# Attention over a 64x64 image on one core: the fifth load of k behind the first energies, the reciprocals' DMA one step later, the sum's halves earlier

## The chip, the cores and the metric

The kernel runs on one core of a Trainium2 chip. The metric is the device time of one execution in microseconds; the kernel before takes 2503.32 us, the median of three runs between 2499.98 and 2505.54. Profiles and traces each show one execution. Engines are named as in the profile: PE is TensorE (its weight loads are PEld), DVE is VectorE, ACT is ScalarE, POOL is GpSimd, SP is SyncE. POOL and SP issue the DMAs; each works through its own instructions in order, as the other engines do.

## The reference

There are 4 images of 64x64 pixels with 256 channels, all float32. The reference computes, for each image, self-attention over N = 4096 positions and adds the input:

```python
q = jnp.einsum('bwhc,cd->bwhd', x, Wq) + bq      # C2 = 128 channels
k = jnp.einsum('bwhc,cd->bwhd', x, Wk) + bk
v = jnp.einsum('bwhc,cd->bwhd', x, Wv) + bv      # C = 256 channels
pq = q.reshape(B, -1, N)                         # the layout is reinterpreted:
pk = k.reshape(B, -1, N)                         # 128 (256 for v) rows of 4096
pv = v.reshape(B, -1, N)
energy = jnp.einsum('bcn,bcm->bnm', pq, pk)
attention = jax.nn.softmax(energy, axis=-1)
out = jnp.einsum('bcm,bnm->bcn', pv, attention)
return gamma * out.reshape(B, W, H, C) + x
```

## The kernel before

**Precision.** Matmuls run on a reduced float32 format (F32R). To keep the precision, each operand of the large matmuls is split in forms: a rounded-down high part h and two remainders l and d, made from the float32 value by one ACT operation and two DVE operations. Each product is then three matmuls. The forms of q and k are written together in a tile f (lines 257 to 263), those of v in vh, vl, vd, those of the exponentials in h and ld.

**Projection.** The work on an image b begins with 16 steps i. A step loads x(i) (L82, on SP, three buffers), transposes it on PE (L123), copies it out of PSUM on ACT (L129), multiplies by Wq and Wk (L136) and Wv (L157), adds the bias of q and k on DVE (L145), makes f by one ACT operation (L259) and two DVE operations (L261), and makes v and its forms (L166, L279 on ACT, L283 on DVE). f has two buffers. POOL stores f to DRAM in three DMAs: kf (L264) and two of qd (L266). From step 3 on, the PSUM tiles of a step (transposes, q and k, v) go round four banks a0, a1, b0, b1.

**The overlap of projection and attention.** The function begin (line 472) puts the first loads and energies of the attention into the later steps of the projection: k_0 to k_4 are loaded back from DRAM by load_k (L296, on POOL, four buffers) at i = 4 to 8, q_0 by load_q (L290) at i = 6, the first energies are at i = 10 to 14. energy(b, 0) at i = 11 is the last reader of k_0, whose buffer k_4 takes.

**Attention.** There are 8 groups g of 512 queries (NG), and for each 16 units t of 256 keys (NU); u = 16 g + t is the unit's number in the image. In its pass of the loop at line 509, unit u issues for other units ahead: cross (one part of the energies, L308, with ACT's L309) of unit u + 3, energy (the rest, L323, and the exponentials L326) and upper (h, L332) of u + 2, load_k of u + 5, halves (DVE: the running sum L341, then L346 and L348 for ld) of u + 1. For itself it issues attend in two halves j of the channels (L365), which add into the four PSUM banks a0, b0, a1, b1: one a and one b for each half.

**The end of a group.** When t = 15, emptied (line 374) copies the four banks to the tile o (L379). sum_forms (line 383) splits the running sum s, which L352 has folded in the unit before, into two forms zf: L388 on ACT, L390 on DVE. finish (line 393) adds them up over the partitions by two matmuls z into bank b0 (L400), copies one row out (L401), and goes on in pieces: each call of proceed() runs every active finish up to its next yield. There is one such call at the end of each unit, and one in each step of the projection. So the finish of an image's last group runs through the next image's projection. Its pieces are: the row to DRAM (L403), back in another shape (L405), the reciprocal and its DMA to DRAM (L407, L408) with the sum of o's two parts (L409), the reciprocals spread to all partitions (L412), a piece with nothing, the multiplication of o (L415), the accumulating load that adds the input (L419, on POOL), a piece with nothing, and the store of the result (L422). L403, L405, L408, L412 and L422 are on SP, as are the loads of x.

The order on each engine is that of the code (manual_schedule); the tiles' dependences set the waits.

Of the kernel before, what the change touches and what calls it, by code (L numbers as in the profile page):

```python
# [13 lines left out]
ALU = mybir.AluOpType  # L14
# [6 lines left out]
def kernel(  # L21
# [36 lines left out]
    nc = tc.nc  # L58
# [118 lines left out]
    NU = NM // 2  # L177
    STEPS = NG * NU
    LOOK = 2
# [19 lines left out]
    with ExitStack() as fast:  # L199
# [26 lines left out]
        def start(pieces):  # L226
            active.append(pieces)
            next(pieces)

        def proceed():  # L230
            for pieces in list(active):
                if next(pieces, StopIteration) is StopIteration:
                    active.remove(pieces)
# [34 lines left out]
        def project_v(b, i):  # L268
            images[b].v(i)
            units[b, "v4", i] = now["v4"]  # L270
            if i < NI - 2:
                for _ in halve_v(b, i):
                    pass
# [14 lines left out]
        def load_q(b, g):  # L288
            t = work.tile([P, NJ, 3, P], F32R, tag="q", name=f"q_{b}_{g}")
            nc.gpsimd.dma_start(t, qd[b, g])  # L290
            loads[b, "q", g] = t

        def load_k(b, u):
            if u < STEPS:
                t = kpool.tile([P, 2, 3, P], F32R, tag="k", name=f"k_{b}_{u}")
                nc.gpsimd.dma_start(t, kf[b, u % NU])  # L296
                loads[b, "k", u] = t

        def forms(b, u, i, f):
            return loads[b, "k", u][:, i, f, :], loads[b, "q", u // NU][:, :, f, :]  # L300

        def cross(b, u):

            if u >= STEPS:
                return
            for i in range(2):
                e = units[b, "e", u, i] = ps_e.tile([P, NB], F32, tag="e", name=f"e_{b}_{u}_{i}")
                nc.tensor.matmul(e, *forms(b, u, i, 2), start=True, stop=False, skip_group_check=True)  # L308
                nc.scalar.mul(e, e, -1.0 / (1.0 + E))  # L309

        def energy(b, u):

            if u >= STEPS:
                return
            if u % NU:
                x = ppool.tile([P, 2, NB], F32, tag="x", name=f"x_{b}_{u}", bufs=3)
            else:
                x = ppool.tile([P, 2, NB], F32, tag="s", name=f"s_{b}_{u // NU}")
            units[b, u] = x
            for i in range(2):  # L320
                e = units.pop((b, "e", u, i))
                for f in range(2):
                    nc.tensor.matmul(  # L323
                        e, *forms(b, u, i, f), start=False, stop=(f == 1), skip_group_check=True
                    )
                nc.scalar.activation(x[:, i, :], e, AF.Exp, scale=(1.0 + E) / E)  # L326

        def upper(b, u):
            if u >= STEPS:
                return  # L330
            h = ppool.tile([P, 2, NB], F32R, tag="h", name=f"h_{b}_{u}", bufs=3)
            nc.scalar.activation(h, units[b, u], AF.Identity, scale=UPPER)  # L332
            units[b, u] = units[b, u], h
# [49 lines left out]
        def sum_forms(b, g):  # L383

            s = now["sum"]
            f = work.tile([P, 2, NB], F32R, tag="r", name=f"zf_{b}_{g}", bufs=1)
            h, l = now["z"] = f[:, 0, :], f[:, 1, :]
            nc.scalar.activation(h, s[:, 0, :], AF.Identity, scale=UPPER)  # L388
            yield
            nc.vector.tensor_tensor(l, s[:, 0, :], h.bitcast(F32), ALU.subtract)  # L390
            yield

        def finish(b, g, o, s):
            n = b * NG + g
            r4 = rall[:, n, :]
            row = lambda t: t[n : n + 1, :]
            spread = lambda t: row(t).rearrange("o (p j) -> (o p) j", j=NJ)
            zp = ps_o.tile([P, NB], F32, tag="b0", name=f"z_{b}_{g}")
            for f, x in enumerate(now["z"]):
                nc.tensor.matmul(zp, ones_r, x, start=(f == 0), stop=(f == 1))  # L400
            nc.scalar.copy(s[0:1, 0, :], zp[0:1, :])  # L401
            yield
            nc.sync.dma_start(row(zd), s[0:1, 0, :])  # L403
            yield
            nc.sync.dma_start(r4, spread(zd))  # L405
            yield
            nc.vector.reciprocal(r4, r4)  # L407
            nc.sync.dma_start(spread(rd), r4)  # L408
            nc.vector.tensor_tensor(o[:, 0], o[:, 0], o[:, 1], ALU.add)  # L409
            yield  # L410
            r = work.tile([P, NB], F32, tag="r", name=f"r_{b}_{g}", bufs=1)
            nc.sync.dma_start(r, rd[n, :].partition_broadcast(P))  # L412
            yield
            yield
            nc.vector.tensor_tensor(  # L415
                o[:, 0], o[:, 0], r.unsqueeze(1).to_broadcast([P, 2, NB]), ALU.mult
            )
            yield
            nc.gpsimd.dma_start(o[:, 0], xg[b, g], accum_op=ALU.add)  # L419
            yield  # L420
            yield
            nc.sync.dma_start(og[b, g], o[:, 0])  # L422
# [48 lines left out]

        def begin(b, i):

            if i in (4, 5, 6, 7, 8):
                load_k(b, i - 4)
            if i == 6:
                load_q(b, 0)
            if i in (11, 13):
                energy(b, (i - 11) // 2)
            if i in (10, 11, 13):  # L480
                cross(b, (i - 9) // 2)
            if i in (12, 14):
                upper(b, i // 2 - 6)

        image(0)
        for b in range(B):
            pr = images[b]
            if b == 0:
                now["banks"] = energies
                pr.transposed(0)  # L490

                wp = ps_o.tile([P, P], F32, tag="b1", name="wp1")
                for _ in range(2):
                    nc.tensor.matmul(wp, ones, ones, start=True, stop=True)
                pr.transposed(1)
                project_qk(b, 0)
            for i in range(1, NI):
                if i == 3:
                    now["banks"] = outputs
                if i + 1 < NI:  # L500
                    pr.transposed(i + 1)
                begin(b, i)
                project_qk(b, i)
                if i == NI - 1:
                    halves(b, 0)
                project_v(b, i - 1)
                proceed()
            project_v(b, NI - 1)
            for u in range(STEPS):
                g, t = divmod(u, NU)  # L510
                final = (b, u) == (B - 1, STEPS - 1)
                if t == 6 and g + 1 < NG:
                    load_q(b, g + 1)
                if u == STEPS - NU and b + 1 < B:
                    image(b + 1)
                if u >= STEPS - 3 and b + 1 < B:
                    now["banks"] = energies
                    if u == STEPS - 3:
                        images[b + 1].load(0)
                    elif u == STEPS - 2:  # L520
                        images[b + 1].transposed(0)
                if (b, u) == (B - 1, STEPS - 6):
                    xr = ppool.tile([P, 2, NB], F32, tag="s", name="xr")
                    nc.sync.dma_start(xr, xg[b, g])

                beside = iter(())
                if u in (2, 6):
                    beside = halve_v(b, NI - 2 + u // 4)
                elif t == NU - 1 and not final:
                    beside = sum_forms(b, g)  # L530
                    total = now["sum"]
                cross(b, u + LOOK + 1)
                if not final:
                    attend(b, u, 0)
                    if t == NU - 1:
                        emptied(b, g, 0)
                energy(b, u + LOOK)
                next(beside, None)
                upper(b, u + LOOK)
                load_k(b, u + LOOK + 3)  # L540
                halves(b, u + 1)
                next(beside, None)
                if final:
                    finish_last(b, u, xr)
                    break
                attend(b, u, 1)
                if t == NU - 1:
                    emptied(b, g, 1)
                    start(finish(b, g, now["o"], total))
                else:  # L550
                    proceed()
            if b + 1 < B:
                images[b + 1].transposed(1)
                project_qk(b + 1, 0)
                proceed()
# [134 lines left out]
```

## Time and profile before

| what | value |
|---|---|
| runs shown | 2503.32 us median, 2499.98 to 2505.54 |
| profiled execution | 2508.35 us, span 2506.6 us |
| busy PE, PEld | 2417.9 us (96%), 1980.8 us (79%) |
| busy DVE, ACT, POOL | 2072.6 us (83%), 1854.0 us (74%), 429.2 us (17%) |
| granted TensorE clock, mean | 0.983 |
| DMA, mean over the span | 135 GB/s |

The span in 40 equal slices shows the four images; a digit is the busy share of a slice in tenths:

```profile
PE   8999999999799999999979999999997999999998
PEclk9999999999899999999989999999998999999999
DMA  8444444443754444444385444444438444444443
```

The dips of PE, and the peaks of DMA, are the four projections, at the slices 1, 11, 21 and 31. The rest is the attention, where PE is busy over 90% of the time. Lines of a timeline give the start in us, the duration in us, the engine, the line and operation, and the tile written and read; in brackets stands the idle time of the engine before and what ended it. A line of stretches gives the stretch and its length, the busy time of PE, PEld, DVE, ACT and POOL (with instructions), the granted clock, the busy share of the DMA engines and GB/s. A line of the waits gives the total in us, the number and the longest.

### The profile page before, as it was taken

What the parts mean: (1) busy time and instruction counts of PE and PEld (TensorE: products, weight loads), DVE (VectorE), ACT (ScalarE), POOL (GpSimd) and SP (SyncE); (2) the same over time, 40 slices, a digit from 0 to 9 for tenths busy, and PEclk for the clock granted to TensorE, in tenths of its full rate; (3) what the DMA queues carried; (4) which work ended last, traced back from release to release, by engine and by line L of the source; (5) the groups of instructions that cost most, each with busy time, mean ns of one, the idle gap of its engine ahead of it and who ended that gap; (6) DMA issues with size and microseconds to landing.
All of it is one profiled execution on the core that took longest, in us unless ns stands there. A gap on an engine that the chain in (4) does not pass through costs nothing.

```text
span 2506.6 us, 30467 instructions
## 1 busy us (share of the span) xinstructions
PE 2417.9 (96%) x10588; PEld 1980.8 (79%) x10588; DVE 2072.6 (83%) x2058; ACT 1854.0 (74%) x3071; POOL 429.2 (17%) x781
## 2 busy tenths in 40 slices
PE   8999999999799999999979999999997999999998
PEld 7788888888678888888867888888886888888886
DVE  5888888888588888888858888888885888888887
ACT  4777777777377777777637777777764777777775
POOL 3211111110321111111032111111113211111110
PEclk9999999999899999999989999999998999999999
DMA  8444444443754444444385444444438444444443
GB/s 244 148 119 121 119 125 119 134 128 98 229 155 120 120 126 118 124 129 128 99 237 151 124 119 123 111 130 124 129 105 241 144 128 126 119 122 116 127 124 90
DMA packets 155215, 338.22 MB, mean 135 GB/s; under 512 B 23471, under 2 KB 56751, under 8 KB 155054
## 3 DMA queue, kind: packets, MB, share of 16 engines
q0 software_dynamic: 114656, 293.52, 43.2%
q1 hardware_dynamic: 39854, 42.41, 5.7%
q8 instruction: 87, 1.43, 0.2%
q14 instruction: 74, 0.61, 0.1%
q10 hardware_dynamic: 544, 0.26, 0.0%
HBM read 268.89 MB, written 67.24 MB: 134 GB/s over the span
## 4 chain that ended last, share of the span: by engine, by line
PE 83%; ACT 6%; issue 4%; DMA 4%; DVE 3%; POOL 1%; SPq 0%; DVEq 0%; ACTq 0%; POOLq 0%
PE a L365 36%; PE b L365 18%; PE e L323 17%; PE e L308 9%; DMA qd<-f 2%; ACT o L379 2%; PE qk L136 1%; ACT v L166 1%; DVE zf L390 1%; ACT x L326 1%; PE v L157 1%; DMA x<-in_x_dram 1%; ACT f L259 1%; ACT zf L388 1%; ACT vh L279 1%
## 5 line engine op out<-in xcount | busy, mean ns | idle before, releaser
L326 ACT ACTIVATE x<-e 128x512 f32<-128x512 f32 x960 | 522.3, 597 | 411.1 <-PE e L323 411.1
L341 DVE TENSOR_TENSOR s<-s,x 128x1024 f32<-128x1024 f32 x480 | 587.2, 1223 | 185.3 <-ACT x L326 179.3
L365 PE MATMUL b<-ld,vd 128*128 128x512 f32 x2048 | 635.0, 391 | 2.2 <-DVE ld L348 2.1
L365 PE MATMUL a<-ld,vl 128*128 128x512 f32 x2048 | 631.5, 390 | 5.5 <-DVE ld L346 5.5
L365 PE MATMUL a<-h,vh 128*128 128x512 f32 x2048 | 632.1, 390 | 0.5 <-ACT v L166 0.5
L346 DVE TENSOR_TENSOR ld<-x,h 128x1024 fp32r<-128x1024 f32 x480 | 584.6, 1218 | 3.0 <-DMA qd<-f 3.0
L348 DVE SCALAR_TENSOR_TENSOR ld<-h,x 128x1024 fp32r<-128x1024 f32 x480 | 584.4, 1218 | 0.0
L296 POOL DMA_DIRECT2D k<-kf x512 | 273.7, 535 | 1765.9 <-PE e L323 1584.8
L323 PE MATMUL e<-q,k 128*128 128x512 f32 x2048 | 550.3, 391 | 0.0
L309 ACT ACTIVATE e<-e 128x512 f32<-128x512 f32 x1024 | 544.0, 564 | 0.9 <-PE e L308 0.8
L332 ACT ACTIVATE h<-x 128x1024 fp32r<-128x1024 f32 x480 | 510.0, 1063 | 14.1
L365 PEld LDWEIGHTS b<-ld,vd 128*128 128x128 f32 x2048 | 382.2, 188 | 92.0 <-ACT s L401 9.9
L365 PEld LDWEIGHTS a<-ld,vl 128*128 128x128 f32 x2048 | 384.4, 188 | 87.1 <-DVE ld L346 7.2
L365 PEld LDWEIGHTS a<-h,vh 128*128 128x128 f32 x2048 | 384.7, 188 | 81.4 <-ACT v L166 1.0
L323 PEld LDWEIGHTS e<-q,k 128*128 128x128 f32 x2048 | 384.7, 188 | 80.3
L308 PE MATMUL e<-q,k 128*128 128x512 f32 x1024 | 318.2, 392 | 0.0
L308 PEld LDWEIGHTS e<-q,k 128*128 128x128 f32 x1024 | 192.7, 189 | 38.6
L261 DVE SCALAR_TENSOR_TENSOR f<-f,qks 128x512 fp32r<-128x512 f32 x128 | 82.8, 688 | 95.8 <-ACT f L259 95.8
L259 ACT ACTIVATE f<-qks 128x512 fp32r<-128x512 f32 x64 | 40.4, 632 | 149.0 <-DMA qd<-f 76.6
L136 PE MATMUL qk<-wqk_sb,xts 128*128 128x256 f32 x512 | 138.5, 419 | 0.1
L157 PE MATMUL v<-xts,wv_sb 128*128 128x256 f32 x512 | 121.9, 383 | 0.0
L136 PEld LDWEIGHTS qk<-wqk_sb,xts 128*128 128x128 f32 x512 | 104.9, 213 | 17.6 <-ACT xts L129 2.1
(68 smaller groups left out, 1063.5 us busy)
## 6 DMA issues: line engine op xcount, KB each, us to landing
k<-kf POOLq DMA_DIRECT2D x512, 384.0 KB, 3.4
kf<-f POOLq DMA_DIRECT2D x64, 384.0 KB, 3.2
qd<-f POOLq DMA_DIRECT2D x128, 192.0 KB, 3.7
q<-qd POOLq DMA_DIRECT2D x32, 768.0 KB, 4.9
x<-in_x_dram SPq DMA_DIRECT2D x64, 256.0 KB, 4.7
o<-in_x_dram POOLq DMA_DIRECT2D x31, 512.0 KB, 6.0
out_dram<-o SPq DMA_DIRECT2D x31, 512.0 KB, 3.1
r<-rd SPq DMA_DIRECT2D x31, 256.0 KB, 4.0
```

The lines of the kernel that those rows point to most:

```text
L136: nc.tensor.matmul(qk[:, s, :], self.xt[i][:, k, s, :], wqk_sb[:, k, :], start=(k == 0), stop=(k == KC - 1),)
L157: nc.tensor.matmul(vp[:, eh, :], wv_sb[:, k, eh * P : (eh + 1) * P], self.xt[i][:, k].rearrange("p s a -> p (s a)"), start=(k == 0), stop= ...
L296: nc.gpsimd.dma_start(t, kf[b, u % NU])
L308: nc.tensor.matmul(e, *forms(b, u, i, 2), start=True, stop=False, skip_group_check=True)
L309: nc.scalar.mul(e, e, -1.0 / (1.0 + E))
L323: nc.tensor.matmul(e, *forms(b, u, i, f), start=False, stop=(f == 1), skip_group_check=True)
L326: nc.scalar.activation(x[:, i, :], e, AF.Exp, scale=(1.0 + E) / E)
L332: nc.scalar.activation(h, units[b, u], AF.Identity, scale=UPPER)
L341: nc.vector.tensor_tensor(s, s, x, ALU.add)
L346: nc.vector.tensor_tensor(l, x, h.bitcast(F32), ALU.subtract)
L348: nc.vector.scalar_tensor_tensor(d, h.bitcast(F32), 1.0 + E, x, ALU.mult, ALU.subtract)
L365: nc.tensor.matmul(to, (vh, vl, vd)[f][:, t + NU * i, j * P : (j + 1) * P], units[b, u][f][:, i, :], start=(t == 0 and i == 0 and f != 1), ...
```

## The change

The change has three parts. In finish, the DMA of the reciprocals moves behind a yield of its own, so it is issued one step later, and every later piece too: what follows on SP, DVE and POOL moves by one unit (or by one step of the projection). The sum of o's parts stays where it was. In begin, load_k(b, 4) moves from i = 8 to i = 12. In the loop over units, sum_forms no longer runs beside the unit in two pieces (L388 behind the exponentials, L390 behind halves), but whole, behind cross and ahead of attend.

```diff
@@ finish
             nc.vector.reciprocal(r4, r4)
+            nc.vector.tensor_tensor(o[:, 0], o[:, 0], o[:, 1], ALU.add)
+            yield
             nc.sync.dma_start(spread(rd), r4)
-            nc.vector.tensor_tensor(o[:, 0], o[:, 0], o[:, 1], ALU.add)
             yield
             r = work.tile([P, NB], F32, tag="r", name=f"r_{b}_{g}", bufs=1)
@@ begin
-            if i in (4, 5, 6, 7, 8):
+            if i in (4, 5, 6, 7):
                 load_k(b, i - 4)
             if i == 6:
                 load_q(b, 0)
...
             if i in (10, 11, 13):
                 cross(b, (i - 9) // 2)
+            if i == 12:
+                load_k(b, 4)
             if i in (12, 14):
                 upper(b, i // 2 - 6)
@@ the loop over units
                 beside = iter(())
                 if u in (2, 6):
                     beside = halve_v(b, NI - 2 + u // 4)
-                elif t == NU - 1 and not final:
-                    beside = sum_forms(b, g)
+                cross(b, u + LOOK + 1)
+                if t == NU - 1 and not final:
                     total = now["sum"]
-                cross(b, u + LOOK + 1)
+                    for _ in sum_forms(b, g):
+                        pass
                 if not final:
                     attend(b, u, 0)
```

## The prediction

> **What bounds the kernel now.** I read first the chain of work that ended last, then the waits by engine, the stretches with the granted clock, and last the order of time around the places that the diff touches.
>
> ```profile
> PE 83%; ACT 6%; issue 4%; DMA 4%; DVE 3%; POOL 1%; SPq 0%; DVEq 0%; ACTq 0%; POOLq 0%
> POOL k L296 <- PE e L308: 63.4, 4, 17.6
> ACT f L259 <- DMA qd<-f: 76.6, 15, 12.7
> PE xt L123 <- DMA x<-in_x_dram: 29.3, 7, 6.1
> SPq L408 <- DVE rall L407: 272.2, 31, 11.9
> SPq L422 <- DMA o<-in_x_dram: 526.3, 31, 18.7
> ```
>
> TensorE carries 83% of the chain; the rest lies in a few places. The wait of POOL on L308 comes four times, once per image, up to 17.6 us. SP's waits are long too, but they matter only where something is queued behind them.
>
> ```profile
> 622.00:712.50 90.50, 73.05 (x330) 61.87 (x330) 51.34 (x94) 44.69 (x89) 28.09 (x52) 0.89 0.72 211
> 720.00:780.00 60.00, 59.75 (x264) 49.16 (x263) 54.45 (x50) 46.76 (x78) 8.12 (x16) 1.00 0.38 110
> ```
>
> In the attention loop (second line) TensorE is full at clock 1.00. In the second image's projection (first line) it works 73 of 90.5 us, part of it at a lowered clock, and the DMA engines are busy 0.72 of the time: 65 us of full traffic, a floor for this stretch. So the change is worth what it does to the four projections.
>
> **The fifth load of k.** Call f(i) the DVE pair L261 of step i, x(i) its load, xt(i) its transposes. POOL issues DMAs in order, and k_4 takes the buffer of k_0, which the first energies (begin, i = 11) read last. Before, k_4 stands ahead of kf_8. In image 2:
>
> ```profile
> 683.51 0.53 POOL L296 DMA_DIRECT2D k<-kf  x1 [17.62 <-PE e L308]
> 690.11 0.63 ACT L259 ACTIVATE f<-qks 128x512 fp32r<-128x512 f32 x1 [12.66 <-DMA qd<-f]
> 691.52 1.12 PE L123 MATMUL xt<-ident,x 128*128 128x128 f32 x4 [4.40 <-ACT v L166]
> ```
>
> POOL sits on k_4, kf_8 and kf_9 sit behind it, f(10) waits 12.7 us for f(8)'s buffer, v(9) waits behind f(10) on ACT, and TensorE for v's bank. After the change k_4 is behind qd_11, when the first energies have been run: no wait, and its user, cross(4) in unit 1, is over 10 us away.
>
> Image 1 has nothing else in it, so it gives the price. f(8) ends at 47.14 + 1.29 = 48.43; its DMAs start 0.5 later, take 1.6 to issue and about 4 to land: 54.5. qks(10) is ready at 53.79 + 0.75 = 54.5, so f(10) starts near 55.3 instead of 62.99: 7.7 us earlier. From there TensorE needs, from xt(12) at 54.01, two steps with energies of 5.26 (54.01 to 59.27), two without of 3.89 (17.69 to 21.58 in this image), 3.46 for the last and 1.74 for its v: 23.5, ending at 77.5 where L308 now starts at 84.63. I take **-7.1**.
>
> **The reciprocals' DMA, one step later, in images 2 to 4.** L408 waits on SP for the reciprocal, and x(5) is behind it; L422 waits for the accumulated DMA of L419, and x(11) is behind that:
>
> ```profile
> 636.84 0.33 SPq L408 DMA_DIRECT2D rd<-rall  x1
> 642.00 1.12 PE L123 MATMUL xt<-ident,x 128*128 128x128 f32 x4 [5.92 <-DMA x<-in_x_dram]
> 668.67 0.59 SPq L422 DMA_DIRECT2D out_dram<-o  x1
> 674.77 1.08 PE L123 MATMUL xt<-ident,x 128*128 128x128 f32 x4 [6.12 <-DMA x<-in_x_dram]
> ```
>
> After it the order on SP is x(5), L408, x(6), L412, x(7), ..., x(11), L422, x(12). The blocks are not gone, they stand ahead of x(6), x(7) and x(12). x(6) is issued near 637.3, lands 4.7 later at 642.0; xt(6) would be due one step after xt(5), near 640. The 2 us are hidden: qk(5) ends at 642 + 0.5 + 1.7 = 644.2, and DVE takes it only at 645.9 by its own pace. x(7), behind L412, is the same, just hidden. L415 moves from between f(5) and f(6) to between f(6) and f(7) (1.13 us of DVE either way), L419 from behind qd_6 to behind qd_7, ahead of kf_8.
>
> So the pace of images 2 to 4 is DVE's: f(i) 4.05 us apart when nothing is late (18.86, 22.91, 26.95, 31.00). f(3) to f(15) takes 72.81, 71.80 and 70.94 us before (639.28 to 712.09; 1264.82 to 1336.62; 1887.68 to 1958.62). After:
> - f(3) to f(4): 4.05, with x(5) in time (8.48, 7.97 and 8.59 before).
> - f(4) to f(11): seven steps, 28.35; L415, 1.13; the energies' ACT work ahead of f(11), 0.31 (4.36 against 4.05); and f(8) waiting for f(6), whose stores queue behind q_0's load: 3.45, from image 1 (39.64 to 47.14 less 4.05). Sum 33.2. The traffic gives nearly the same: x 1.8, f 5.5, k 1.6, q 0.8, o 0.5, out 0.5, r 0.3 = 11.0 MB, at 340 GB/s (34 to 47 us, DMA share 1.11) 32.4 us. I take 33.5.
> - f(11) to f(15): as now, 16.95, 17.05, 16.51.
>
> Sums 54.5, 54.6, 54.1: 18.3, 17.2 and 16.8 us less. Off that goes about 1 us because TensorE ends after DVE (as in image 1) and 1 for x(12): L419 issued at f(7)'s stores, near 660, lands 6.8 later, x(12) 5.3 after that, near 672.5, some 2 us after xt(12) is due. I take -16.3, -15.2, -14.8: **-46**. Bounds: -20 each if no wait is left; -8 each if x(12) costs TensorE all that x(11) did (6.1 idle and some 2 of lowered clock).
>
> The clock matters for the short waits that stay. After 4.40 idle it was 0.50 (692 to 697), after 0.99 it stayed 1.00, after 2.64 (to 47.89) it was 0.66 from 48 to 53, a loss of 1.7 us. I put nothing into the sum for two such waits in three images; by the row of 2.64 it would be up to +10, which the range holds. The Trainium skill ("TensorE: Matmul & The Clock Gate", section "Part 1: The HAM clock gate") lets the clock fall after an idle window of about 3.4 us, free-running; by that rule waits of 2 us cost no clock. The row of 2.64 disagrees.
>
> **The sum's halves, made early.** ACT's L388 moves ahead of the L379 pair and the exponentials of a group's last unit, DVE's L390 ahead of L346 and L348.
>
> ```profile
> 222.55 0.49 PE L400 MATMUL z<-zf,ones 128*128 128x512 f32 x1
> 223.28 0.50 PE L400 MATMUL z<-zf,ones 128*128 128x512 f32 x1 [0.23 <-DVE zf L390]
> 224.47 0.56 ACT L401 COPY s<-z 1x512 f32<-1x512 f32 x1
> 225.07 0.30 PEld L365 LDWEIGHTS b<-ld,vd 128*128 128x128 f32 x2 [0.34 <-ACT s L401]
> ```
>
> TensorE loses about 1.1 us here: a group lasts 66.87 (151.85 to 218.80 in the chain), 16 units of 4.08 are 65.3, the two z 0.45. The wait for zf goes. But b0, z's bank, is free only after L401 at 225.03, and ACT runs from 216.57 to 225.97 without a gap, with the same work in either order. TensorE reaches L365 b at 224.08 and waits there 1 us: the stall moves, it doesn't shrink. **0** for 28 boundaries; bounds -31 (1.1 each) and +14 (0.5 each, should the later L348 reach TensorE: it ends near 223.2 instead of 221.1, and b needs it at 225.1). At the three ends of an image with another behind it ACT waits 3.09 us for TensorE before L379, so zf costs it nothing, the two z follow at 620.8 instead of 621.0 and 621.7, and xt(1) starts at 621.3 instead of 622.1: -0.8 each, **-2.4**.
>
> Inside an image L408's DMA keeps its time (SP has nothing else), and L415 and L419 come a unit later; DVE has 0.58 idle in a unit, no k load waits for them that is due within two units: 0.
>
> **Sum:** -7.1 - 46 - 2.4 = -55.5. The profiled execution took 2508.35 (span 2506.6), 5 over the median 2503.3 of the runs; so 2453 for it and **2448** for the median.
>
> **Rivals.**
> 1. The projection runs into its DMAs or keeps its x waits, x(6) or x(12), at full size with the slow clock. For it: the DMA share is 0.98 to 1.09 from 642 to 674. Against it: in image 1 three steps from 22 to 34, at share 1.01, kept 4.05. About -9 for each of three images, -5 for the first: -32, **2471**. The Trainium skill ("DMA: Bandwidth & Descriptors", section "Where 436 GB/s comes from") puts memory's side at some 358 GB/s per core: 11.0 MB would take an estimated 31 us, so by it this rival is no likelier.
> 2. f's buffers keep up everywhere and image ends gain: 20 in three images, 7.7 and 2.4: -70, **2433**.
> 3. Slower: DVE's L390 in front of L346 and L348 holds up unit 16's ld at all 28 boundaries. DVE stands still until ACT has made zf; if ACT took zf only after the exponentials, as now, L348 would end near 225.5, and b would wait 0.4 for it. It decides from 227.2 on, 2.1 us past the point where b needs it, for only then do 28 boundaries eat the 55 and 5 more: **2508**. Against it: L352 ends at 217.7 and ACT has only L309 ahead of L388, so zf is due at 220.3.
> 4. It does nothing, because f(10) waits for something other than the stores behind k_4: 2503. Against it: ACT names the DMA, and image 1 shows it alone.
>
> **Chances.** Forecast 0.52, rival 1 0.26, rival 2 0.17, rival 3 0.03, rival 4 0.02. No change means within 0.2% (5 us), about what a measurement of this kernel can tell. Faster 0.95, same 0.02, slower 0.03. The range 2431 to 2475 reaches to rivals 1 and 2 and the extra clock loss.
>
> **What would show it.** POOL's wait on L308 and ACT's 12 us at L259 gone in all four images; f(3) to f(15) near 54.5; image 1's first L308 of unit 3 at 77 to 78; xt(5) without a wait, xt(12) with about 2 us; at boundaries the waits before L400 gone and L365 b waiting about 1 us for L401. Wrong: a new wait of 5 us or more at xt(6) or xt(12), f(8) or f(9) waiting over 5 us for their DMAs, or a boundary other than 1.6 us over 16 units.

## The result, and the profile after

The changed kernel takes 2466.02 us, the median of four runs between 2465.25 and 2466.45, against 2501.65 for the kernel before in the same comparison: a ratio of 0.9855 with a 95% interval of 0.9838 to 0.9872. That is 36 us less, where 55 had been forecast; 2466 lies inside the range, nearer to the prediction's first rival (2471) than to its forecast (2448). The profiled executions are further apart, 2508.35 and 2466.14 us (spans 2506.6 and 2464.4), since the one of before lies 5 to 7 us above its median; the places below are compared in these two traces, 42.2 us apart.

Three views of the kernel after follow. The first gives the shares of the chain that ended last, by engine; the second some of its waits (total, number, longest); the third the second image's projection as one stretch (PE, PEld, DVE, ACT, POOL busy; clock, DMA share, GB/s).

```profile
PE 80%; ACT 11%; DMA 4%; DVE 2%; issue 1%; POOL 0%; SPq 0%; ACTq 0%; DVEq 0%; POOLq 0%
```

```profile
ACT f L259 <- DMA qd<-f: 36.8, 15, 4.3
PEld b L365 <- ACT s L401: 36.6, 28, 1.3
PE b L365 <- ACT s L401: 24.4, 28, 0.9
PE xt L123 <- DMA x<-in_x_dram: 21.7, 8, 7.2
```

```profile
612.00:691.50 79.50, 69.48 (x330) 59.42 (x329) 51.03 (x94) 45.10 (x89) 28.10 (x52) 0.94 0.80 239
```

POOL's wait on L308 is gone, and ACT's longest wait at L259 has fallen from 12.7 to 4.3 us. The projection lasts 79.5 us instead of 90.5, with the DMA engines busier (0.80). Two lines show what stayed: TensorE now waits 28 times for L401, once at each group end inside an image, and it still waits for x, once for 7.2 us.

The place of that wait in image 2, in the order of time:

```profile
626.99 0.33 SPq L410 DMA_DIRECT2D rd<-rall  x1
631.91 0.63 PE L123 MATMUL xt<-ident,x 128*128 128x128 f32 x4 [1.06 <-DMA x<-in_x_dram]
638.83 0.63 PE L123 MATMUL xt<-ident,x 128*128 128x128 f32 x4 [2.83 <-DMA x<-in_x_dram]
653.34 1.13 POOL L420 DMA_DIRECT2D o<-in_x_dram  x1
659.80 0.59 SPq L423 DMA_DIRECT2D out_dram<-o  x1
666.30 1.09 PE L123 MATMUL xt<-ident,x 128*128 128x128 f32 x4 [5.67 <-DMA x<-in_x_dram]
669.75 2.45 PE L136 MATMUL qk<-wqk_sb,xts 128*128 128x256 f32 x8
677.07 0.54 POOL L296 DMA_DIRECT2D k<-kf  x1
```

xt(5) has no wait any more; xt(6) and xt(7) have short ones. SP stands at the store L423 until the load L420 has landed, x(12) is behind it, and TensorE waits 5.67 us at xt(12). In images 3 and 4 that wait is 7.21 and 3.68 us; for the last of them the view names ACT's L279 in place of x, but it went, too, when the store was moved (below). The multiplication L136 behind it takes 2.45 us, against 1.89 at full clock. k_4 is issued at 677.07 with nothing to wait for.

### The profile page after: what moved, and what is told of

Its sections match the earlier page's. It is cut to its first block, busy times and chain, and to the rows that moved or that the text cites. A ratio compares the mean times of both kernels' runs of the same rounds, so it can differ in the third digit from the quotient of the medians.

```text
span 2464.4 us, 30518 instructions
## 1 busy us (share of the span) xinstructions
PE 2391.0 (97%) x10588; PEld 1973.5 (80%) x10588; DVE 2072.6 (84%) x2058; ACT 1856.3 (75%) x3071; POOL 429.3 (17%) x781
## 4 chain that ended last, share of the span: by engine, by line
PE 80%; ACT 11%; DMA 4%; DVE 2%; issue 1%; POOL 0%; SPq 0%; ACTq 0%; DVEq 0%; POOLq 0%
PE a L365 33%; PE b L365 18%; PE e L323 17%; PE e L308 8%; DMA qd<-f 3%; ACT o L379 3%; ACT h L332 2%; PE qk L136 2%; ACT s L326 1%; ACT x L326 1%; PE v L157 1%; DMA x<-in_x_dram 1%; ACT e L309 1%; ACT v L166 1%; ACT f L259 1%
## 5 line engine op out<-in xcount | busy, mean ns | idle before, releaser
L365 PE MATMUL b<-ld,vd 128*128 128x512 f32 x2048 | 634.6, 391 | 27.1 <-ACT s L401 24.4
L365 PE MATMUL a<-ld,vl 128*128 128x512 f32 x2048 | 631.8, 390 | 3.9 <-DVE ld L346 3.9
L365 PE MATMUL a<-h,vh 128*128 128x512 f32 x2048 | 632.1, 390 | 0.5 <-ACT v L166 0.5
L348 DVE SCALAR_TENSOR_TENSOR ld<-h,x 128x1024 fp32r<-128x1024 f32 x480 | 585.2, 1219 | 0.0
L365 PEld LDWEIGHTS b<-ld,vd 128*128 128x128 f32 x2048 | 381.5, 188 | 119.6 <-ACT s L401 36.6
L365 PEld LDWEIGHTS a<-ld,vl 128*128 128x128 f32 x2048 | 384.4, 188 | 85.6 <-DVE ld L346 5.6
L365 PEld LDWEIGHTS a<-h,vh 128*128 128x128 f32 x2048 | 384.2, 188 | 81.8 <-ACT v L166 1.0
L308 PE MATMUL e<-q,k 128*128 128x512 f32 x1024 | 318.0, 392 | 0.0
L308 PEld LDWEIGHTS e<-q,k 128*128 128x128 f32 x1024 | 192.8, 189 | 40.0
L261 DVE SCALAR_TENSOR_TENSOR f<-f,qks 128x512 fp32r<-128x512 f32 x128 | 82.8, 689 | 60.4 <-ACT f L259 60.4
L136 PE MATMUL qk<-wqk_sb,xts 128*128 128x256 f32 x512 | 127.2, 393 | 0.6 <-ACT xts L129 0.5
L259 ACT ACTIVATE f<-qks 128x512 fp32r<-128x512 f32 x64 | 40.4, 630 | 110.6 <-DVE qks L145 73.8
L157 PEld LDWEIGHTS v<-xts,wv_sb 128*128 128x128 f32 x512 | 98.3, 192 | 15.7 <-PE qk L136 2.0
```

Source lines behind the costliest of these rows:

```text
L136: nc.tensor.matmul(qk[:, s, :], self.xt[i][:, k, s, :], wqk_sb[:, k, :], start=(k == 0), stop=(k == KC - 1),)
L157: nc.tensor.matmul(vp[:, eh, :], wv_sb[:, k, eh * P : (eh + 1) * P], self.xt[i][:, k].rearrange("p s a -> p (s a)"), start=(k == 0), stop= ...
L348: nc.vector.scalar_tensor_tensor(d, h.bitcast(F32), 1.0 + E, x, ALU.mult, ALU.subtract)
L365: nc.tensor.matmul(to, (vh, vl, vd)[f][:, t + NU * i, j * P : (j + 1) * P], units[b, u][f][:, i, :], start=(t == 0 and i == 0 and f != 1), ...
```

## The experiments

f(i) is the DVE pair L261 of step i, as in the prediction. Medians are compared with the kernel before on the same chip, 2504.5 to 2504.7 in the three comparisons. Where a kernel is said to be below the kernel after, it is the difference of the two medians. The kernel after stands in a comparison of its own, in which the kernel before took 2501.65, so such a difference is uncertain by some 3 us.

### The three parts alone

The change has three parts; each was put alone into the kernel before. Only the load:

```diff
-            if i in (4, 5, 6, 7, 8):
+            if i in (4, 5, 6, 7):
                 load_k(b, i - 4)
...
+            if i == 12:
+                load_k(b, 4)
```

> Only the fifth load of k is moved. Theory A (the projections gain from k_4 alone, and x(11) stays blocked behind the store L422): image 1 as with the whole change, its projection 6.9 us shorter and the start of its attention 2.9; in images 2 to 4 x(5) and x(11) still come late, but f(9) to f(10) falls from 18.4, 17.6 and 16.6 us to about 11, so 6 to 8 us each. Sum about -30, median near 2472. Theory B (the yield made the gain of images 2 to 4): only image 1 gains, about -10, median near 2492.

Measured: 2482.83, ratio 0.9907 (0.9889 to 0.9925), -22 us: about midway between the two. The trace sides with A's mechanism: in images 2 to 4 f(3) to f(15) fell by 7.1, 6.0 and 4.3 us, where A had 6 to 8 each and B nothing. f(9) to f(10) fell to 9.7, 9.8 and 9.6 us, further than expected, but f(10) to f(11) grew to 5.3 to 5.4 from 4.4. x(5) and x(11) came as late as before, which TensorE's waits in image 2 show:

```profile
634.66 1.11 PE L123 MATMUL xt<-ident,x 128*128 128x128 f32 x4 [6.33 <-DMA x<-in_x_dram]
667.86 1.09 PE L123 MATMUL xt<-ident,x 128*128 128x128 f32 x4 [7.43 <-DMA x<-in_x_dram]
```

Only the step of the reciprocals' DMA:

```diff
             nc.vector.reciprocal(r4, r4)
-            nc.sync.dma_start(spread(rd), r4)
             nc.vector.tensor_tensor(o[:, 0], o[:, 0], o[:, 1], ALU.add)
             yield
+            nc.sync.dma_start(spread(rd), r4)
+            yield
```

> Only the reciprocals' DMA and what follows it move one step. Theory A: x(5) comes in time, which saves some 3.5 us at f(4) in images 2 to 4, but POOL still stands at k_4, and that wait ends only when the first energies have run behind xt(12), which now waits for x(12) behind the store; what f(4) gains is given back: between -10 and 0, median 2491 to 2502. Theory B: -25, median near 2477.

Measured: 2488.06, ratio 0.9934 (0.9914 to 0.9954), -16.6 us: neither. What f(4) gained (4.4, 3.9 and 4.5 us) was not given back behind k_4: f(9) to f(10) took 15.5, 15.9 and 15.7 us instead of 18.4, 17.6 and 16.6. The two parts add for the most part: in the three images together f(3) to f(15) fell by 17.4 us with the load alone, 17.7 with the step alone and 30.2 with both, 5 less than the sum.

Only the sum's halves:

```diff
-                elif t == NU - 1 and not final:
-                    beside = sum_forms(b, g)
+                cross(b, u + LOOK + 1)
+                if t == NU - 1 and not final:
                     total = now["sum"]
-                cross(b, u + LOOK + 1)
+                    for _ in sum_forms(b, g):
+                        pass
```

> Only the halves of the running sum are made early. Theory A (ACT has no idle time there, the stall of TensorE moves from L400 to L365 b behind L401): at group ends 0.06 to 0.08 us longer each, at the three image ends 0.8 shorter: between -2 and +3 in all, median 2500 to 2505. Theory B (the waits at z were a loss of their own): -1.1 us at 28 boundaries, -31, median near 2471.

Measured: 2503.16, ratio 0.9994 (0.9985 to 1.0004). Theory A: no time of its own. TensorE's waits for zf are gone, and waits of 24.2 us in all at L365 b for L401 stand there instead, as in the kernel after (24.4).

### What holds x(12): the store moved behind the last x

```diff
             nc.gpsimd.dma_start(o[:, 0], xg[b, g], accum_op=ALU.add)
-            yield
-            yield
+            for _ in range(6 if g == NG - 1 else 2):
+                yield
             nc.sync.dma_start(og[b, g], o[:, 0])
```

> The whole change, and in the finish of an image's last group the store of the result is four steps later, behind the last x on SP. Theory A (x(12) was late only because SP stood at the store): TensorE's waits of 5.7, 7.2 and 3.7 us at xt(12) go, and the lowered clock behind them; f(10) to f(11) falls from 11.2, 11.7 and 9.1 to 4.4 to 5: 16 to 19 us less than the whole change, median near 2448. Theory B (the DMA engines are full there, share 1.0, and x(12) or f's buffers would be late anyway): less than 6 us, median above 2460.

Measured: 2450.33, ratio 0.978 (0.9763 to 0.9797), some 16 us below the kernel after. Theory A holds: f(10) to f(11) is 4.36, 4.36 and 4.53 us instead of 11.19, 11.70 and 9.06. In image 2 TensorE goes on without a wait for x(12), and waits 0.33 us for ACT; the store follows later:

```profile
661.17 0.60 PE L123 MATMUL xt<-ident,x 128*128 128x128 f32 x4
662.11 1.22 PE L323 MATMUL e<-q,k 128*128 128x512 f32 x4 [0.33 <-ACT e L309]
662.40 0.67 SPq L423 DMA_DIRECT2D out_dram<-o  x1
```

Whether the other two short waits are worth removing too:

```diff
+            if g == NG - 1:
+                yield
             nc.sync.dma_start(spread(rd), r4)
...
-            yield
-            yield
+            for _ in range(5 if g == NG - 1 else 2):
+                yield
             nc.sync.dma_start(og[b, g], o[:, 0])
```

> The whole change, and in the finish of an image's last group the reciprocals' DMA one step later still and the store behind the last x, so that x(6), x(7) and x(12) are not behind a waiting DMA on SP. Theory A: no wait of TensorE for x above 1 us in images 2 to 4; besides the wait at xt(12) also those at xt(6) (1.1, 0.2, 0.6) and xt(7) (2.8, 1.7, 2.5) go; f(3) to f(15) falls from 61.9, 63.4 and 60.1 us to about 54: 18 to 26 us less than the whole change, median 2440 to 2448. Theory B (the DMA engines' traffic is the bound of steps 4 to 10): f waits for its stores instead, f(3) to f(15) stays above 58: less than 10 us.

Measured: 2455.47, ratio 0.9803 (0.9787 to 0.9819), 10.6 us below the kernel after: just outside theory B's range, far from A's, and not better than moving the store alone (the median is 5 us higher, but the intervals overlap). f(3) to f(15) took 56.8, 56.8 and 57.5 us, between the two theories. TensorE has no waits for x left in the projections, but ACT's waits at L259 for f's buffers are 57.1 us, against 36.8 in the kernel after and 42.3 with the store alone (the first line is the store alone, the second this kernel):

```profile
ACT f L259 <- DMA qd<-f: 42.3, 15, 5.0
```

```profile
ACT f L259 <- DMA qd<-f: 57.1, 19, 4.6
```

So in steps 4 to 10 the next limit, the wait for f's stores, is close behind the x loads. This kernel also differs from the one with the store alone by the input's load, which the extra yield moves from step 7 to step 8. f(10) to f(11) takes 6.55, 6.45 and 7.10 us in it, against 4.36 to 4.53 there: f(11) waits for f(9)'s stores, which now run beside that load. So this run doesn't price the waits at xt(6) and xt(7) by themselves.

### The group end: z and its copy earlier

```diff
-                attend(b, u, 1)
                 if t == NU - 1:
-                    emptied(b, g, 1)
+                    attend(b, u, 1, (0, 1))
                     start(finish(b, g, now["o"], total))
+                    attend(b, u, 1, (2,))
+                    emptied(b, g, 1)
                 else:
+                    attend(b, u, 1)
                     proceed()
```

> The whole change, and in a group's last unit the two matmuls z and the copy L401 stand ahead of the second half's b matmuls and of the second pair of L379, so that ACT reaches L401 some 1.15 us earlier. Theory A (TensorE waits at L365 b for L401 because of what stands ahead of it on ACT): the wait of 0.87 us at 28 boundaries shrinks to 0.3 or less: 15 to 24 us less than the whole change, median 2442 to 2451. Theory B (ACT's sum of work sets the boundary, whatever its order): TensorE then waits as long at another place, within 5 us of the whole change, median 2461 to 2471.

Measured: 2440.42, ratio 0.974 (0.9723 to 0.9756), 26 us below the kernel after: theory A, and a little more than its upper end. L401 now stands ahead of the second pair of L379, and TensorE goes from z to the next unit's b without a wait (ACT, then PE, in the order of time; lines between these are left out):

```profile
215.41 0.56 ACT L401 COPY s<-z 1x512 f32<-1x512 f32 x1
215.88 0.68 ACT L379 ACTIVATE o<-a,gam 128x512 f32<-128x512 f32 x1
```

```profile
213.83 0.62 PE L400 MATMUL z<-zf,ones 128*128 128x512 f32 x2
214.29 0.63 PE L365 MATMUL b<-ld,vd 128*128 128x512 f32 x2
216.14 0.63 PE L365 MATMUL b<-ld,vd 128*128 128x512 f32 x2
216.61 1.09 PE L323 MATMUL e<-q,k 128*128 128x512 f32 x4
```

A group takes 65.96 us (211.66 to 277.62 at L388) against 66.95 after (208.25 to 275.20 at h): 0.99 less, at 28 group ends 28 us, of which the medians show 26.

### Both together

> Both of the two above together. Theory A: they lie in different stretches (group ends; projections), so they add: 33 to 48 us less than the whole change, median 2418 to 2433. Theory B of either: one of them is missing from the sum.

Here the group end's edit stands beside the one that frees x(6), x(7) and x(12). Measured: 2431.63, ratio 0.9708 (0.9693 to 0.9723), 34 us below the kernel after: they add. With the store alone instead:

> The whole change with the store behind the last x and z early. Theory A (projection and group ends are separate): the 16 us of the one and the 25 us of the other add, median 2423 to 2429. Theory B (the start of a projection hangs on the group end before it, so that they share): above 2431.

Measured: 2423.19, ratio 0.9677 (0.9664 to 0.9691), 43 us below the kernel after. Theory A.

### What holds the projection then

Two further kernels took traffic out of the busiest steps, each on top of the one before. First the loads of k, then the input's accumulating load (with it the store of the result goes from step 13 to step 14):

```diff
-            if i in (4, 5, 6, 7):
+            if i in (4, 5):
                 load_k(b, i - 4)
+            if i == 9:
+                load_k(b, 2)
...
-            if i == 12:
-                load_k(b, 4)
+            if i in (12, 13):
+                load_k(b, i - 9)
```

> As the one before, and the loads k_2, k_3 and k_4 stand at steps 9, 12 and 13 instead of 6, 7 and 12, where the DMA engines are less busy. Theory A (after the store is out of the way, steps 5 to 10 are held by the DMA traffic, through f's two buffers): f(5) to f(9) wait less, f(3) to f(15) falls by 1.5 to 3 us in each image, 6 to 12 us in all. Theory B (f waits for the latency of its own three stores, whatever else is on the DMA engines): within 3 us of the one before.

```diff
-            yield
+            for _ in range(6 if g == NG - 1 else 1):
+                yield
             nc.gpsimd.dma_start(o[:, 0], xg[b, g], accum_op=ALU.add)
-            for _ in range(6 if g == NG - 1 else 2):
-                yield
+            yield
+            yield
             nc.sync.dma_start(og[b, g], o[:, 0])
```

> As the one before, and the accumulating load of the input, of the last group of an image, stands five steps later, at step 12 instead of 7, and the store two steps after it. Theory A (traffic): another 1.5 to 3 us in each of images 2 to 4, 4 to 9 us. Theory B: within 3 us.

Measured: 2422.27 (ratio 0.9672, 0.9659 to 0.9685) and 2427.74 (0.9694, 0.9681 to 0.9707). The first is no different, as theory B had it; the second is not faster but 5 us slower in the median, which neither had. The two intervals overlap slightly, but the slowest run of the first (2424.68) is faster than the fastest of the second (2426.93). The traces show that waits moved. Where the input's load left step 7, f(9) to f(10) fell from 6.1, 5.5 and 6.2 us to 4.05 in all three images; where it went, f(14) to f(15) grew from 4.05 to 5.2, 5.3 and 5.9, and TensorE's wait for ld at the start of the attention grew as well. The projections of images 2 to 4 (from the last z to the first L365) became 0.8, 0.4 and 1.6 us shorter, but the attentions became longer, that of image 4 by 3.2 us up to its last z, the other three by 0.8 to 1.4. The page's waits of the first kernel, then of the second:

```profile
ACT f L259 <- DMA qd<-f: 41.6, 16, 3.8
PE a L365 <- DVE ld L346: 6.0, 4, 2.7
```

```profile
ACT f L259 <- DMA qd<-f: 38.9, 14, 3.8
PE a L365 <- DVE ld L346: 9.8, 4, 4.8
```

So f's stores near the moved load were late again: f(15) waits for those of f(13), and ld, which shares its two buffers with f, for those of f(14). Whether the input's load or the result's store delays them, the run doesn't show, since both moved. Whether a third buffer for f would help was not tried. The fastest kernel tried is thus the whole change with the store behind the last x and z early, without these two: 2423 us (2422 with the loads spread, which is not distinguishable).

## Why the prediction was right, and where it was off

**The mechanism was right in the load of k and at the group ends, and right by half in the reciprocals' DMA.** Of the three parts, POOL's block at k_4 was the largest loss (22 us alone), and it is gone in all four images; x(5) is in time; the group ends cost nearly the same. The direction is as forecast, and the median is inside the range. But the range had been drawn to reach the first rival, and what happened at x(12) is what that rival had: the number doesn't confirm the sum. Two of the prediction's own signs failed as well. It named a new wait of 5 us or more at xt(12) as a sign of being wrong, and that wait was 5.7 and 7.2 us in images 2 and 3; and f(3) to f(15) took 61.9, 63.4 and 60.1 us instead of about 54.5.

**The sum was too large.** By the places in the two traces (the first L308 of unit 3, then xt(1) of the next image):

| stretch | forecast | measured |
|---|---|---|
| projection 1 | -7.1 | -6.9 |
| attention 1, with its image's end | -0.8 | -2.9 |
| projections 2, 3, 4 | -16.3, -15.2, -14.8 | -10.9, -10.0, -10.8 |
| attention 2 to 4, with two image ends | -1.6 | -0.7 |
| sum (-55.5 in the prediction's rounding) | -55.8 | -42.2 |

**The step that failed** is the term "1 for x(12)" in the sum of images 2 to 4. f(10) to f(11) took 6.8, 7.3 and 4.7 us more than the 4.36 it takes when nothing is late: some 19 where 3 had been put. Moving the store away gave 16 back, and that kernel, at -54, is where the forecast of -55 had been: its projections 2 to 4 (last z to first L365) are 16.6, 15.8 and 15.9 us shorter than before, where 16.3, 15.2 and 14.8 had been forecast. The agreement is close, but in part luck: f(3) to f(15) fell by 46.1 us in all in that kernel, where the sum had 52.3 before it took off 6 for TensorE's end and x(12). The price was wrong for two reasons, shown here for image 2. The wait of 3.45 for f's buffer had been placed at f(8), but its time was spent sooner: f(5) and f(6) waited for their buffers and came 0.7 and 1.5 us late, f(7), behind xt(7), another 0.9 beside the multiplication of o. So f(4) to f(7) took 16.5 us instead of 13.3, f(7) to f(8) 4.05. The sum from f(4) to f(10), 29.0, was as forecast (28.9), but L420 stands behind f(7)'s stores and left with them, some 3 us later than worked out, and TensorE waited 5.7 us for x(12), not 2. And after that idle time the clock was low, so xt(12), the energies and qk(11) took 5.9 us (666.30 to 672.20), against 4.3 with the store moved away (661.17 to 665.51). The granted clock was 0.57 in the stretch around them:

```profile
664.00:672.00 8.00, 5.70 (x18) 4.84 (x19) 1.19 (x2) 2.76 (x5) 1.58 (x3) 0.57 0.88 276
```

**The rivals.** The first had this, x(12) at its full size with the slow clock, and its 2471 lies nearer than the forecast. Its other half, the DMA traffic, was not what stopped the kernel after, since the store's move alone gave 16 us. The experiments show waits for f's stores as the next limit; how much of them is traffic stays open, since spreading the loads of k gained nothing. The 340 and 358 GB/s that the prediction reckoned with were no upper bound: from 639 to 644 the DMA engines moved 392. The second (no wait left) was ruled out by f's stores: in images 2 to 4 f(3) to f(15) stays at 55.7 to 57.8 us with the store moved and at 56.8 to 57.5 with all of x free, against the 54.5 of the forecast and the 48.6 of twelve steps of 4.05. The third did not happen: at the group ends TensorE's b waits for L401, not for L348. The fourth fell with the trace of the load alone: image 1's f(9) to f(10) went from 11.8 to 5.6 us.

**The group ends** came out as worked out: TensorE's wait is 0.87 us at L365 b instead of about 1.1 around L400, and a group takes 66.95 instead of 66.88 (154.97 to 221.85 at L388). The two ends that the prediction gives for a group are 66.95 apart, not 66.87, which changes nothing in its sum. What the forecast called a fixed sum of ACT's work was a matter of order after all: putting L401 ahead of two copies that are needed later freed bank b0 in time, and saved 0.99 us per group.

**Attention 1** gained 2.1 us more than the image's end. In the kernel before TensorE waited 2.71 us for ld there and then ran at a lower clock (0.66 in the 5 us from 88.6); after, it waits 1.18, and the clock stays 1.00.

## What to carry to other kernels

When an in-order queue blocks on a DMA that must wait, moving that DMA one place chooses which load stands behind it, and the wait can come back there; ask for every later item of the queue what will be late next, with its time counted from the events it really follows, and move the waiting item behind the last load that others need. When a wait moves from one line to another without getting shorter, look at what stands ahead of the releasing instruction on its engine: its order may be the whole cost. Price a wait together with what runs slower after it.

## What the runs showed of the hardware

The clock often fell after short idle times, but the length of the idle time alone didn't decide it. In the kernel after, TensorE idled 2.83 us ahead of xt(7) in image 2 and 2.46 in image 4, and the granted clock was 0.66 and 0.70 in the 5 us that followed; after 1.65 us in image 3 it stayed 1.00. In image 1 of the same kernel it fell to 0.66 (48 to 53) after only 1.90 us. The other way round, with the store alone moved, it stayed 1.00 behind 3.24 us of idle time (image 4, ahead of 1856.75). The clearest pair is in the last kernel, whose input's load is late: ahead of xt(7) TensorE idled 2.85 us in image 2 and 2.84 in image 3, and the clock in the 5 us behind was 0.66 (from 632.5) and 1.00 (from 1234.9). What else decides it, no run here shows. The stretches of the kernel after, image 3 first, then 4, then 2:

```profile
1250.00:1254.00 4.00, 3.83 (x20) 3.38 (x21) 1.32 (x3) 2.05 (x5) 0.17 (x1) 1.00 1.09 336
1866.00:1871.00 5.00, 5.00 (x20) 4.27 (x19) 3.34 (x6) 2.56 (x6) 2.65 (x5) 0.70 1.18 393
639.00:644.00 5.00, 5.00 (x18) 4.10 (x18) 2.78 (x6) 1.73 (x3) 2.64 (x5) 0.66 1.18 392
```

The Trainium skill ("TensorE: Matmul & The Clock Gate", section "Part 1: The HAM clock gate") names an idle window of about 3.4 us, free-running. The falls here came after shorter idle times, as after the 2.64 us of the kernel before, and the measured rows decide.
